# The last expert of a two-layer decoder in a written order: way back between the down products, final norm on ScalarE, stores of two batches

## The chip, the cores and the metric

The kernel runs on one core of a Trainium2 chip. The core has a matrix engine (TensorE, PE in the profile; its weight loads are listed as PEld), VectorE (DVE), ScalarE (ACT), GpSimd (POOL), and SyncE (SP), whose queue issues almost all DMA transfers here. The metric is the device time of one execution in microseconds (us), as the median of the runs; less is better.

## The reference

The input is 16 batches of 128 tokens with 256 features. Two decoder layers follow one another, each of three blocks (attention or mixture, cross attention, feed forward), and each block ends in `x = layernorm(x + block(x))`. The change is in the last block, a mixture of eight experts in which every expert picks its own tokens:

```python
logits = jnp.einsum('bsd,ed->bse', x, gate_w)
affinity = jnp.transpose(jax.nn.softmax(logits, axis=-1), (0, 2, 1))
gating, idx = jax.lax.top_k(affinity, k)              # k = S // E * CAPACITY = 32 tokens per expert and batch
x_in = x[bidx, idx]
h = jax.nn.silu(jnp.einsum('bekd,eid->beki', x_in, w_gate)) * jnp.einsum('bekd,eid->beki', x_in, w_up)
x_e = jnp.einsum('beki,edi->bekd', h, w_down)
out = jnp.zeros_like(x).at[bidx, idx].add(gating[..., None] * x_e)
...
x = _layernorm(x + out)      # mean and variance over the 256 features, eps 1e-5
```

## The kernel before

The last stage computes in float32, and the 16 tiles `x[b]` (128 tokens by 256 features) stay in SBUF for the whole kernel. `stage5` (line 2484) is the last stage. Its input `xin` holds, for each expert, the 512 picked tokens (32 of each of 16 batches), features on the partitions.

One expert goes as follows. `Results.hidden` (line 2456) runs eight times, once per 128 of the 1024 hidden units: products with the gate and up weights into the PSUM tiles `ps_g` and `ps_m` (line 2462), a SiLU on ScalarE (line 2466) and a product on VectorE (line 2467) that leaves `h`. `Results.down` (line 2469) runs four times, once per group g of four batches: eight matmuls over the hidden units into `ps_y` (line 2473), a copy to `y` on ScalarE (line 2474), and four small DMAs (line 2481). The rows of `y` are 4 batches by 32 tokens; the DMAs put the 32 rows of each batch into a tile `res.y[g]`, in which four experts come to lie above one another on the 128 partitions (they share the tag `ring` with other tiles, so the profile calls them `ring`).

The *way back* adds the experts' results to the tokens that they came from. For each batch one matmul with a gated one-hot matrix (`r.back`, called `half` in the profile) sums four experts at once into `ps_o` (line 2523), and VectorE adds it to `x[b]` (line 2524). It is done after expert 3 for experts 0 to 3 and after expert 7 for experts 4 to 7. After expert 7 each batch is then normed and stored: `K.layernorm` (line 85) takes statistics and their sum on VectorE (lines 88 and 90), the root on GpSimd in two instructions (lines 82 and 83, the second a power of -0.5), and scales on VectorE (line 93) into `o`; line 2528 stores `o` with a DMA of 128 KB per batch.

A float32 matmul of 128 by 256 shows as two MATMUL records in the trace, each with its weight load. I call one such record a pass.

What sets the order: outside of a block `tc.manual_schedule()` a scheduler of the framework orders the instructions of each engine by its own costs, and inside it they are issued as written. Each engine and the SP queue then work strictly in that order. `stage5` is scheduled by the framework before the change; the order that it chose puts the 32 down products of expert 7 first, then the 16 way-back products, and mixes adds, statistics and norms on VectorE. Tiles of one tag share a fixed number of buffers: `ps_o`, `ps_y`, `ps_g` and `ps_m` have two each, `o` two, `y` four.

Of the kernel before, what the change touches and what calls it, by code (L numbers as in the profile page):

```python
# [8 lines left out]
F32 = mybir.dt.float32  # L9
# [4 lines left out]
AF = mybir.ActivationFunctionType  # L14
ALU = mybir.AluOpType
# [4 lines left out]
P = 128  # L20
NB = 16
D = 256
# [5 lines left out]
class Kernel:  # L28
# [43 lines left out]
    def rows(self, pool, name, n):  # L72

        t = self.new(pool, [P, n], F32, name)
        self.nc.sync.dma_start(t, self.ins[name].partition_broadcast(P))
        return t
# [34 lines left out]
NE = 8  # L111
# [7 lines left out]
def stage0(K, early, ahead, late, late_dram, context):  # L119
# [8 lines left out]
    with ExitStack() as ctx:  # L128
# [560 lines left out]
        for n in range(N + 2):  # L689
# [24 lines left out]
            if mid:  # L714
                down(n - 1)
                factor(n - 1)
# [1609 lines left out]
TOK = 32  # L2326
FI = 1024


def load5(K, e, tile):  # L2330

    w = SimpleNamespace()
    w.gate, w.up, w.down = [], [], []
    for i, (n, dst) in enumerate((("l1f_gateT", w.gate), ("l1f_upT", w.up))):
        for k in range(KD):
            t = tile(2 * i + k, [P, FI])
            K.nc.sync.dma_start(t, K.ins[n][e][k * P:(k + 1) * P, :])
            dst.append(t)
    for i in range(2):
        t = tile(4 + i, [P, 4, D])  # L2340
        K.nc.sync.dma_start(t, K.ins["l1f_downT"][e].rearrange("(k p) n -> p k n", p=P)[:, 4 * i:4 * i + 4, :])
        w.down.append(t)
    return w
# [106 lines left out]
class Results:  # L2450
# [18 lines left out]
    def down(self, w, e, g, pd, y, rows):  # L2469

        K, nc = self.K, self.K.nc
        for c in range(FI // P):
            nc.tensor.matmul(pd, rows(c), w.down[c // 4][:, c % 4, :], start=(c == 0), stop=(c == FI // P - 1))  # L2473
        nc.scalar.copy(y, pd)  # L2474
        if e % 4 == 0:
            if g == 0:
                self.y = []
            self.y.append(K.new(self.ring, [P, 4, D], F32, "ring"))
        at = slice(e % 4 * TOK, e % 4 * TOK + TOK)
        for i in range(4):  # L2480
            nc.sync.dma_start(self.y[g][at, i, :], y[i * TOK:i * TOK + TOK, :])


def stage5(K, r, res, wp, first, out, ring):


    tc, nc = K.tc, K.nc
    x = K.x
    with ExitStack() as ctx:
        work = ctx.enter_context(tc.tile_pool(name="s5_work", bufs=2))  # L2490
        small = ctx.enter_context(tc.tile_pool(name="s5_small", bufs=4))
        ps = ctx.enter_context(tc.tile_pool(name="s5_ps", bufs=2, space=PSUM))


        def tile_of(i, shape):
            return K.new(wp, shape, F32, f"w5_{i}")

        weights = [first, load5(K, 1, tile_of)]
        for e in range(NE):
            w = weights[e]  # L2500
            hid = []
            n = 2 if e == 0 else 1
            wide = NB * TOK // n
            for c in range(0, FI // P, n):
                pg, pu = (K.new(ps, [P, n, wide], F32, t) for t in ("ps_g", "ps_m"))
                h = K.new(work, [P, n, wide], F32, "h", bufs=12)
                res.hidden(w, e, range(c, c + n), slice(NB * TOK - wide, NB * TOK), pg, pu, h)
                hid += [h[:, j, :] for j in range(n)]
            if e + 2 < NE:
                weights.append(load5(K, e + 2, tile_of))  # L2510
            for g in range(4 - 4 // n, 4):
                y = K.new(work, [P, D], F32, "y", bufs=4)
                at = (g - 4 + 4 // n) * P
                res.down(w, e, g, K.new(ps, [P, D], F32, "ps_y"), y, lambda c: hid[c][:, at:at + P])
            if e == 0:
                for g in range(4):
                    r.ways(g, small, ps, ring)
            if e % 4 < 3:
                continue
            for b in range(NB):  # L2520
                g, i = divmod(b, 4)
                po = K.new(ps, [P, D], F32, "ps_o")
                nc.tensor.matmul(po, r.back[g][:, i, e // 4, :], res.y[g][:, i, :], start=True, stop=True)
                nc.vector.tensor_tensor(x[b], x[b], po, ALU.add)
                if e == NE - 1:
                    o = K.new(work, [P, D], F32, "o")
                    K.layernorm(small, o, x[b])
                    nc.sync.dma_start(out[b], o)

# [1 line left out]
def decoder(tc, ins, out):  # L2533
    with ExitStack() as ctx:
# [5 lines left out]
        with ExitStack() as until4:  # L2540
# [37 lines left out]
            first = stage4(K, w.four, w.kv, r5, res)  # L2578
        p5 = pool(ctx, "w_5", bufs=2)
        stage5(K, r5, res, p5, first, out, w.kv.ring)  # L2580


# [60 lines left out]
```

## Time and profile before

| what | us |
|---|---|
| median of 3 runs | 1392.26 (1391.93 to 1396.34) |
| profiled execution, its own time | 1398.93 |
| its span, first to last instruction | 1397.1 |
| around the span (difference of the two) | 1.83 |
| mean granted TensorE clock | 0.957 |
| PE busy | 1231.7 (88%) |
| VectorE busy | 834.5 (60%) |
| ScalarE busy | 666.8 (48%) |
| GpSimd busy | 477.8 (34%) |

The profile is of one execution, 6.67 us longer than the median of the runs. Times in the timeline count from the first instruction. Busy shares are means over all stages, and say little of the last 40 us, which the change is in; those are read from the timeline, the chain of work that ended last, and tables by window. "Granted clock" is the share of full speed that the matrix engine was given in a window.

### The profile page before, as it was taken

How to read it: one execution, taken by the hardware profiler on the slowest of the kernel's cores; microseconds unless marked ns; L12 is line 12 of the kernel's file. 1: busy time of each engine (PE TensorE's matmuls, PEld its weight loads, DVE VectorE, ACT ScalarE, POOL GpSimd, SP SyncE). 2: the span in 40 equal slices, each digit the busy share in tenths (PEclk: the TensorE clock that was granted, in tenths of full speed). 3: DMA queues.
4: the chain of work that ended last, by engine and by line, in shares of the span. 5: the costliest groups of instructions: out<-in, count | busy, mean ns of one | idle time of the engine just before them, and what ended most of it. 6: DMA issues, size and time to landing. Idle time of an engine off the chain costs nothing.

```text
span 1397.1 us, 19300 instructions
## 1 busy us (share of the span) xinstructions
PE 1231.7 (88%) x6779; PEld 849.2 (61%) x6791; DVE 834.5 (60%) x1778; ACT 666.8 (48%) x1713; POOL 477.8 (34%) x642
## 2 busy tenths in 40 slices
PE   3688987889978999878898999998999999999995
PEld 1455444666654667656555788877777655666553
DVE  7899978989957898757444566667333111211115
ACT  5789865778956566543122665654521111111110
POOL 4256557668852776420042232332202000000003
PEclk9899988989999999997799999998999999999998
DMA  9368324111011211102000212211005222233002
GB/s 321 125 190 295 109 79 81 16 39 31 32 53 56 69 60 53 46 24 68 1 0 11 82 62 76 61 61 46 1 8 188 77 94 77 69 106 104 9 9 75
DMA packets 63121, 103.55 MB, mean 74 GB/s; under 512 B 11920, under 2 KB 41712, under 8 KB 62768
## 3 DMA queue, kind: packets, MB, share of 16 engines
q1 hardware_dynamic: 60848, 96.76, 20.8%
q0 software_dynamic: 2176, 5.55, 1.9%
q8 instruction: 54, 0.88, 0.3%
q14 instruction: 43, 0.35, 0.1%
HBM read 81.74 MB, written 16.35 MB: 70 GB/s over the span
## 4 chain that ended last, share of the span: by engine, by line
PE 52%; DVE 29%; ACT 7%; POOL 5%; issue 4%; DMA 2%; another core or an unknown queue 0%; SPq 0%; DVEq 0%; POOLq 0%; ACTq 0%
PE ps_y L2473 7%; PE ps_m L2462 7%; PE ps_g L2462 7%; PE ps_m L2018 4%; DVE acc L1307 3%; ACT s L2120 2%; PE ps_t L2140 2%; PE ps_m L2149 2%; PE ps_m L2038 2%; DVE cT L1316 2%; DVE s L915 1%; DVE m L2114 1%; DVE s L2110 1%; PE ps_t L2129 1%; PE ps_s L2107 1%
## 5 line engine op out<-in xcount | busy, mean ns | idle before, releaser
L2467 DVE TENSOR_TENSOR h<-h,ps_m 128x512 f32<-128x512 f32 x60 | 41.3, 688 | 228.4 <-PE ps_m L2462 228.4
L82 POOL TENSOR_SCALAR ln_t<-ln_mv 128x1 f32<-128x1 f32 (+1 forms) x84 | 16.4, 195 | 449.7 <-DVE ln_mv L90 308.4
L2120 ACT ACTIVATE s<-s,m 128x128 f32<-128x128 f32 x256 | 99.3, 390 | 69.1 <-DVE m L2114 69.1
L2466 ACT ACTIVATE h<-ps_g 128x512 f32<-128x512 f32 x60 | 35.8, 597 | 171.0 <-PE ps_g L2462 171.0
L2462 PE MATMUL ps_g<-xin,w 128*128 128x512 f32 x224 | 106.3, 592 | 0.0
L2462 PE MATMUL ps_m<-xin,w 128*128 128x512 f32 x224 | 105.3, 592 | 0.0
L2473 PE MATMUL ps_y<-w,h 128*128 128x256 f32 x448 | 97.8, 379 | 0.0
L2473 PEld LDWEIGHTS ps_y<-w,h 128*128 128x128 f32 x448 | 85.1, 190 | 14.6 <-issue 3.3
L2124 POOL TENSOR_TENSOR s<-s,t 128x1024 f32<-128x1024 f32 x32 | 60.7, 1896 | 91.1 <-DVE t L2123 91.1
L927 ACT ACTIVATE s<-s,m 128x128 f32<-128x128 f32 x256 | 83.2, 394 | 11.7 <-DVE m L922 11.7
L2462 PEld LDWEIGHTS ps_m<-xin,w 128*128 128x128 f32 x224 | 42.5, 190 | 51.4 <-issue 50.2
L2462 PEld LDWEIGHTS ps_g<-xin,w 128*128 128x128 f32 x224 | 42.0, 190 | 46.4 <-issue 45.0
L2018 PE MATMUL ps_m<-xT,half 128*128 128x256 f32 x256 | 62.5, 389 | 2.6 <-DVE qT L2023 1.9
L2474 ACT COPY y<-ps_y 128x256 f32<-128x256 f32 x30 | 11.2, 372 | 104.7 <-PE ps_y L2473 70.8
L2110 DVE TENSOR_TENSOR s<-ps_s,hide 128x1024 f32<-128x1024 f32 x32 | 39.2, 1224 | 35.9 <-PE ps_s L2107 35.9
L2149 PE MATMUL ps_m<-half,oT 128*128 128x256 f32 x256 | 59.3, 385 | 0.0
L1307 DVE SCALAR_TENSOR_TENSOR acc<-ps_m,l1a_conv_w,acc 128x508 f32<-128x508 f32 (+2 forms) x72 | 53.3, 740 | 3.0 <-ACT acc L1300 1.3
L2018 PEld LDWEIGHTS ps_m<-xT,half 128*128 128x128 f32 x256 | 47.4, 194 | 9.1 <-DVE qT L2023 2.3
L2149 PEld LDWEIGHTS ps_m<-half,oT 128*128 128x128 f32 x256 | 47.4, 190 | 7.5
L83 POOL TENSOR_TENSOR ln_rs<-ln_t,mhalf 128x1 f32<-128x1 f32 (+1 forms) x84 | 48.6, 578 | 7.0
L2120 ACT ACTIVATION_READ_ACCUMULATOR s<-s,m 128x1 f32 x256 | 48.1, 188 | 0.0
L1298 PE MATMUL ps_m<-xnT,l1a_in_proj 128*128 128x512 f32 x96 | 46.8, 611 | 0.4 <-ACT y L1268 0.4
(524 smaller groups left out, 3079.2 us busy)
## 6 DMA issues: line engine op xcount, KB each, us to landing
w<-in_w_gate_dram SPq DMA_DIRECT2D x9, 1024.0 KB
csb<-cs_dram SPq DMA_DIRECT2D x16, 512.0 KB
w<-in_l1f_gateT_dram SPq DMA_DIRECT2D x14, 512.0 KB
w<-in_l1f_upT_dram SPq DMA_DIRECT2D x14, 512.0 KB
w<-in_l1f_downT_dram SPq DMA_DIRECT2D x14, 512.0 KB
k<-kv SPq DMA_DIRECT2D x20, 256.0 KB
v<-kv SPq DMA_DIRECT2D x20, 256.0 KB
ring<-k SPq DMA_DIRECT2D x10, 512.0 KB
```

The source lines that it names most:

```text
L83: return self.nc.gpsimd.tensor_tensor(out, t, self.mhalf[: out.shape[0], :n], ALU.pow)
L927: nc.scalar.activation(at, at, AF.Exp, bias=m[h][:, i:i + 1])
L1298: nc.tensor.matmul(pc, w.inp[:, k, at:at + P], xnT[g][:, k, :], start=(k == 0), stop=(k == KD - 1))
L1307: nc.vector.scalar_tensor_tensor(accv[:, :, j:], pcv[:, :, :P - j], w.conv[:, c, TAPS - 1 - j:TAPS - j], accv[:, :, j:], ALU.mult, ALU.add,)
L2018: nc.tensor.matmul(pq[:, j, :], wt[k][:, at], src[:, k, :], start=(k == 0), stop=(k == KD - 1))
L2110: nc.vector.tensor_tensor(half(b, j), pss.rearrange("p r c k -> p (r c) k"), hide.unsqueeze(1).to_broadcast([P, 8, P]), ALU.add,)
L2120: nc.scalar.activation(at, at, AF.Exp, bias=m[j][:, i:i + 1], accum_out=t[j][:, i:i + 1])
L2124: nc.gpsimd.tensor_tensor(half(b, j), half(b, j), t[j].unsqueeze(2).to_broadcast([P, 8, P]), ALU.mult)
L2149: nc.tensor.matmul(py[b], oT[b][:, c, :], w.o[c // 4][:, c % 4, :], start=(c == 0), stop=(c == NC - 1))
L2462: nc.tensor.matmul(ps[:, j, :], m[k][:, c * P:(c + 1) * P], self.r.xin[:, k, e, cols], start=(k == 0), stop=(k == KD - 1),)
L2467: nc.vector.tensor_tensor(h, h, pu, ALU.mult)
L2473: nc.tensor.matmul(pd, rows(c), w.down[c // 4][:, c % 4, :], start=(c == 0), stop=(c == FI // P - 1))
```

## The change

The last expert leaves the loop and is written out in a block with a manual schedule. `Results.down` is split in two, of which the second half (`moved`) holds the four DMAs, without a change in what they do. The loop over the first seven experts keeps its text, and the way back of experts 0 to 3 stays where it was.

For the last expert, the order of groups is written by hand: the way back and the statistics of a group of four batches (`back`) stand behind the down products of the next group. The statistics of two batches go into one tile `ln_mv2`, and GpSimd computes the roots of two batches at once, then minus mean times root (two more instructions). ScalarE scales (`normed`) with the root as scale and that product as bias, instead of VectorE. Results of two batches lie in one `o` with four buffers, stored with one DMA of 256 KB (`stored`). For the last group, `begun` puts `x[b]` into PSUM with a product by the identity before the group's own down results have come, `back` adds the way back in the same PSUM tile, and statistics and scaling read PSUM; the add on VectorE is left out for these four batches.

```diff
-        for e in range(NE):
+        for e in range(NE - 1):
...
+        with tc.manual_schedule():
+            w, hid, po, o, todo = weights[NE - 1], [], {}, {}, []
...
+            def begun(g):
+                for b in range(4 * g, 4 * g + 4):
+                    po[b] = K.new(ps, [P, D], F32, "ps_g" if b % 2 else "ps_m")
+                    nc.tensor.matmul(po[b], K.ident, x[b], start=True, stop=False)
+
+            def back(g):
+                for i in range(4):
+                    b = 4 * g + i
+                    there = b in po
+                    if not there:
+                        po[b] = K.new(ps, [P, D], F32, "ps_o")
+                    nc.tensor.matmul(po[b], r.back[g][:, i, 1, :], res.y[g][:, i, :], start=not there, stop=True)
+                    if not there:
+                        nc.vector.tensor_tensor(x[b], x[b], po[b], ALU.add)
+                    of = po[b] if there else x[b]
+                    st = K.new(small, [P, 6], F32, "ln_st")
+                    nc.vector.bn_stats(st, of)
+                    if i % 2 == 0:
+                        mv = K.new(small, [P, 2, 2], F32, "ln_mv2")
+                    nc.vector.bn_aggr(mv[:, i % 2, :], st)
+                    if i % 2:
+                        rs, nb = (K.new(small, [P, 2], F32, t) for t in ("ln_rs2", "ln_nb2"))
+                        K.rsqrt(small, rs, mv[:, :, 1:2].rearrange("p h c -> p (h c)"), 1.0, 1e-5, "ln_t2")
+                        nc.gpsimd.tensor_tensor(nb, mv[:, :, 0:1].rearrange("p h c -> p (h c)"), rs, ALU.mult)
+                        nc.gpsimd.tensor_scalar(nb, nb, -1.0, None, ALU.mult)
+                        todo.append((b // 2, [po[b - 1 + j] if there else x[b - 1 + j] for j in range(2)], rs, nb))
+
+            def normed(g):
+                for _ in range(2):
+                    n, of, rs, nb = todo.pop(0)
+                    o[n] = K.new(work, [P, 2, D], F32, "o", bufs=4)
+                    for j in range(2):
+                        nc.scalar.activation(o[n][:, j, :], of[j], AF.Identity, scale=rs[:, j:j + 1], bias=nb[:, j:j + 1])
+
+            def stored(g):
+                for i in (2 * g, 2 * g + 1):
+                    nc.sync.dma_start(out[2 * i:2 * i + 2].rearrange("b p d -> p b d"), o[i])
+
+            down(0)
+            down(1)
+            back(0)
+            down(2)
+            normed(0)
+            back(1)
+            stored(0)
+            down(3)
+            normed(1)
+            back(2)
+            normed(2)
+            stored(1)
+            begun(3)
+            back(3)
+            stored(2)
+            normed(3)
+            stored(3)
```

More of the change, by code (lines that the diff above doesn't have):

```diff
@@ L2474, in down, with moved @@
         nc.scalar.copy(y, pd)
+        self.moved(e, g, y)
+    def moved(self, e, g, y):
+        K, nc = self.K, self.K.nc
         if e % 4 == 0:
@@ L2517, in stage5 @@
                     r.ways(g, small, ps, ring)
[L2518 to L2528, printed above, removed]
+            if e == 3:
+                for b in range(NB):
+                    g, i = divmod(b, 4)
+                    po = K.new(ps, [P, D], F32, "ps_o")
+                    nc.tensor.matmul(po, r.back[g][:, i, 0, :], res.y[g][:, i, :], start=True, stop=True)
+                    nc.vector.tensor_tensor(x[b], x[b], po, ALU.add)
@@ new lines, in stage5, with down @@
+        with tc.manual_schedule():
+            w, hid, po, o, todo = weights[NE - 1], [], {}, {}, []
+            for c in range(FI // P):
+                pg, pu = (K.new(ps, [P, 1, NB * TOK], F32, t) for t in ("ps_g", "ps_m"))
+                h = K.new(work, [P, 1, NB * TOK], F32, "h", bufs=12)
+                res.hidden(w, NE - 1, range(c, c + 1), slice(0, NB * TOK), pg, pu, h)
+                hid.append(h[:, 0, :])
+            def down(g):
+                y = K.new(work, [P, D], F32, "y", bufs=4)
+                res.down(w, NE - 1, g, K.new(ps, [P, D], F32, "ps_y"), y, lambda c: hid[c][:, g * P:(g + 1) * P])
+            def begun(g):
[49 more added lines that the diff above has]
+            stored(3)
```

## The prediction

> **What bounds the kernel now.** I read first the busy time in three windows of the last stage: the down products of expert 7, the way back, and what comes after the last matmul. Columns are busy time and instructions of each engine, granted clock, and DMA share.
>
> ```profile
> 1356.00:1370.60 14.60, 14.60 (x68) 12.47 (x67) 0.69 (x1) 1.12 (x3) 0.00 (x0) 1.00 0.09 25
> 1370.60:1386.00 15.40, 10.69 (x33) 5.75 (x31) 13.32 (x49) 0.37 (x1) 9.28 (x24) 0.89 0.24 80
> 1386.00:1397.00 11.00, 0.00 (x0) 0.00 (x0) 4.76 (x16) 0.00 (x0) 3.18 (x8) 0.67 0.28 96
> ```
>
> For 14 us only PE works; then VectorE (third figure) is nearly full for 15 us, and for 11 us more PE has nothing to do. Next I read the chain of work that ended last, over the same stretch (start, us, what).
>
> ```profile
> 1356.93 13.81 PE ps_y L2473 x64
> 1370.74 0.45 PE ps_o L2523 x2
> ...
> 1385.18 0.47 DVE ln_st L88 x2
> ...
> 1386.51 1.67 DMA out_dram<-o
> 1388.28 0.42 DVE o L93
> 1388.72 1.68 DMA out_dram<-o
> 1390.49 0.42 DVE o L93
> 1390.93 1.68 DMA out_dram<-o
> 1392.74 0.42 DVE o L93
> ```
>
> So the end is PE for 13.8 us, VectorE for some 15 us, then norms that each wait until an older store has landed and given back one of the two `o`. The last norm ends at 1393.67, the last store is issued at 1393.92 and lands at 1396.02, and closing work runs 1.05 us to 1397.07. Last, the groups of this stretch by form (busy, mean ns).
>
> ```profile
> L2473 PE MATMUL ps_y<-w,h 128*128 128x256 f32 x64 | 14.0, 379 | 0.0
> L2523 PE MATMUL ps_o<-ring,half 128*128 128x256 f32 x32 | 10.7, 459 | 4.7 <-DVE x L2524 4.6
> L83 POOL TENSOR_TENSOR ln_rs<-ln_t,mhalf 128x1 f32<-128x1 f32 x16 | 9.2, 573 | 1.3
> L93 DVE TENSOR_SCALAR o<-x,ln_mv,ln_rs 128x256 f32<-128x256 f32 x16 | 6.3, 407 | 4.1 <-DMA out_dram<-o 2.6 <-POOL ln_rs L83 1.3
> L2524 DVE TENSOR_TENSOR x<-x,ps_o 128x256 f32<-128x256 f32 x16 | 6.3, 396 | 13.7 <-PE ps_o L2523 13.7
> L88 DVE BATCH_NORM_STATS2 ln_st<-x 128x6 f32<-128x256 f32 x16 | 6.1, 407 | 0.0
> ```
>
> Matmuls overlap: 64 passes in 13.81 us are 0.2157 us each, whatever their 379 ns.
>
> **The change part by part.** The order in which the changed program issues its work is the same as before on every engine up to the down products of expert 7, and no table load is added on ScalarE. So everything up to 1363.68, the end of the second group's passes, is taken as it is, and I work forward from there.
>
> *Way back between the downs.* The results of group 0 are there: its four DMAs were issued from 1360.86 to 1362.68 and land 1.77 to 1.89 us later, at 1362.63, 1363.30, 1363.88 and 1364.52. Two matmuls go at once (two `ps_o`), 4 passes, 0.86 us. The third needs the first add: it comes 0.64 us after the matmul's start, takes 0.42, and PE follows 0.05 us later. The fourth needs the second add, and VectorE now has the statistics of one batch between two adds. A batch there is add 0.42 + 0.03, statistics 0.43 + 0.04, aggregate 0.08 until the next instruction starts (steps of dependent instructions at 1387.22 and at 699.28 of the timeline), 1.0 us. Fourth matmul at 0.64 + 1.0 + 0.42 + 0.05 = 2.11 us, its two passes 0.54 after a pause: 2.65 us per group of which 1.73 are passes. VectorE needs 4.0 us of each 6.1 us, so it isn't the bound. The sum on PE:
>
> - back(0) to 1366.33, down(2) with 16 passes (3.45) to 1369.78, back(1) to 1372.44, down(3) to 1375.89, back(2) to 1378.55.
> - begun(3), 8 passes that the old kernel doesn't have, 1.73, to 1380.27. It is covered: the last of the four DMAs of group 3 lands at 1375.67 + 0.46 (until ScalarE's copy) + 0.40 + 3.68 = 1380.21. Without it PE would wait about as long.
> - back(3) to 1382.0 in 8 passes, nothing to wait for but the matmuls before.
>
> *What is late next.* The adds of the last four batches are gone (4 x 0.42, paid for by begun(3)). Statistics run from 1380.9, 0.55 a batch, and end at 1383.2. GpSimd becomes the bound: for two batches it has 0.19 (line 82), the power, a product 0.20 and a scaling 0.19 (rows of 128 by 4: 199 and 193 ns), with 0.08 between two. The power of 128 by 2 is on no row; 128 by 1 takes 0.55, 128 by 4 takes 1.04. I take 0.71, on the line between them. That is 1.61 us for a pair from start to start. The sixth pair's statistics are there at 1380.54, so three pairs in a row end at 1380.63 + 3 x 1.61 - 0.08 = 1385.38, where VectorE alone would allow 1384.8.
>
> *ScalarE.* Two scalings of 128 by 256 with a scale per partition: rows between 372 ns (line 2474) and 489 ns (line 568), which start 0.31 to 0.42 us apart. I take 0.87 for two, to 1386.29. The other twelve lie under PE's work: normed(0) takes 1370.4 to 1372.1, before the copy of group 3 at 1376.13, which waits behind it on the same engine.
>
> *Stores.* SP has stored(0) ahead of group 3's four DMAs. It is done by some 1373.6, and SP needs them at 1376.5. With four `o` of two batches no scaling waits for a store. The last store carries 256 KB: stores of 128 KB land after 1.67 to 2.09 us, those of `k` with 256 KB after 2.00 to 2.64 us. I take 2.05. Another price stands in the Trainium skill ("DMA: Bandwidth & Descriptors", section on the anatomy of one DMA on the software path): 2.0 us plus the bytes over 436 GB/s, which is an estimated 2.6 us here and would make the sum 0.55 us less. It gives 2.3 for 128 KB, and these stores, on the hardware path, took 1.67 in most cases, so the row decides.
>
> **Sum**: 1386.29 + 0.03 + 2.05 + 1.05 = 1389.4 against 1397.1: 7.7 us less. The profiled execution would go from 1398.93 to 1391.2; its distance to the median, 6.67 us, lies mostly before this stage and stays. So 1392.26 - 7.7 = **1384.6**.
>
> Bounds: a group's way back on PE 2.4 to 2.9 (three of them, -0.75 to +0.75); the power 0.55 to 1.04 for three pairs (-0.5, then VectorE is the bound, to +1.0); the two small GpSimd steps up to 0.05 more each (+0.3); statistics from PSUM, for which there is no row: adds that read PSUM take 396 ns and statistics that read SBUF 407, so nothing to 0.1 each, hidden under GpSimd; two scalings 0.75 to 0.95 (+-0.1); the store 1.67 to 2.64 (-0.4 to +0.6). Together 5.0 to 9.4 us, so 1382.9 to 1387.3.
>
> **Rivals.** *The clock falls between the groups.* The clock goes in windows of 3.41 us.
>
> ```profile
> 1369.33:1372.74 3.41, 3.33 (x15) 2.26 (x13) 1.51 (x6) 0.37 (x1) 0.00 (x0) 1.00 0.14 39
> 1372.74:1376.15 3.41, 0.87 (x4) 0.38 (x3) 2.14 (x9) 0.00 (x0) 1.75 (x6) 1.00 0.21 67
> 1376.15:1379.57 3.42, 3.17 (x7) 1.89 (x8) 3.23 (x13) 0.00 (x0) 2.35 (x6) 0.50 0.27 94
> 1379.57:1382.98 3.41, 2.58 (x10) 1.40 (x9) 3.41 (x14) 0.00 (x0) 2.71 (x7) 1.00 0.29 100
> ```
>
> After a window with 4 passes and a pause of 2.2 us the next one got half the clock; after 7 and 10 passes the next was full. The new order has at least 8 passes in 2.65 us and 3.5 more of the downs, 11 a window, and no pause over 0.5 us. A DMA or add that is late by 2 us would break that. Each fallen window costs up to 1.7 us. Two of them: 1384.6 + 3.4 = 1388.0, at the edge of what can be told from no change.
>
> *The clock stays at half from the first way back on.* This is the case that ends slower. From 1363.68 PE has 72 passes, 15.5 us, which become 31.1, and the pauses (2.8 us) vanish in them: the last matmul 12.7 us later, GpSimd no longer the bound (-0.6): 1384.6 + 12.1 = 1396.7. It decides from five of the six windows on (5 x 1.7 over 7.7). The Trainium skill ("TensorE: Matmul & The Clock Gate", section on a second failure mode, by cycling PSUM buffers) says that short pauses between groups of matmuls can make the clock fall and rise again and again, which speaks against this order. The rows above don't show it: with pauses as short and fewer passes the clock came back and stayed.
>
> *A queue in front.* ScalarE does normed(0) before it copies group 3's `y`, and that copy releases the DMAs that back(3) needs. If the roots of pair 1 (1369.97 by my sum) came over 4 us late, all that follows would move with them; no row of GpSimd comes near that. A gain halved by such shifts: 1388.5.
>
> *More than forecast.* If PE doesn't pause in a group at all (1.73 instead of 2.65 us, three times) and the power costs as for one batch: 1384.6 - 2.8 - 0.5 = 1381.3. Against it stands that PE did wait for the adds before (4.6 us in the group row of line 2523).
>
> **How the numbers follow.** My forecast (1381.5 to 1387.5) 0.76; two windows of half clock or a gain halved by a queue 0.14; more than forecast, under 1381.5, 0.06; half clock throughout 0.04. What this kernel's measurement can tell from no change is about 0.3%, 4.2 us, so 1388.1 and 1396.4. Faster: 0.76 + 0.06 + half of 0.14 = 0.89, less 0.02 for the spread of the runs shown (their highest is 4.1 us over the median): 0.87. Same: 0.09. Slower: 0.04. Range 1381.5 to 1388.5, which takes in the bounds and half of the first rival.
>
> **What would show it.** Right: on PE some 2.65 us of way back after each of downs 1, 2 and 3; the last matmul ends near 1382.4, not 1386; no scaling waits for a store; GpSimd's eight powers of 128 by 2 at about 0.7 us, the last three pairs without a pause; last store issued near 1386.3; span near 1389.4. Wrong: half the clock in a window from 1366 on; PE waiting for a DMA at back(3); group 3's copy late behind the scalings; a power over 1.04 us.

## The result, and the profile after

| | before | after |
|---|---|---|
| median of 20 runs each, us | 1400.54 (1391.93 to 1410.26) | 1394.78 (1385.83 to 1401.72) |
| profiled execution: its own time, its span | 1398.93, 1397.1 | 1389.15, 1387.4 |
| mean granted clock in it | 0.957 | 0.961 |
| first down pass of the last expert, to the end of the span | 1356.77, 40.35 us | 1353.24, 34.20 us |

The ratio of the times is 0.9953, with a 95% interval of 0.9931 to 0.9974. By this ratio the kernel is 6.6 us faster (3.6 to 9.7), where 7.7 was forecast. But the predicted time of 1384.6 is missed by 10 us, and 1394.78 lies outside the range: the kernel before, with 1392.26 from three runs, has a median of 1400.54 over 20.

First the busy time of the changed kernel in three windows: the downs of the first groups with the first way back, the middle, and what is left from 1377.40 on (busy time and instructions of PE, PEld, DVE, ACT and POOL, then the granted clock, the DMA share and GB/s).

```profile
1353.24:1367.00 13.76, 13.39 (x61) 11.04 (x59) 4.60 (x14) 1.27 (x4) 2.65 (x8) 1.00 0.07 19
1367.00:1377.40 10.40, 9.60 (x42) 7.29 (x41) 7.44 (x25) 4.79 (x11) 4.13 (x13) 1.00 0.25 78
1377.40:1387.44 10.04, 1.22 (x6) 0.74 (x4) 2.07 (x8) 3.60 (x7) 3.75 (x12) 0.73 0.45 158
```

Before, VectorE had almost nothing to do during the downs and was nearly full during the way back. Now it works beside PE in the first two windows, and PE keeps the full clock up to its last passes. Then the chain of work that ended last (start, us, what).

```profile
1353.40 6.91 PE ps_y L2473 x32
1360.31 0.45 PE ps_o L2555 x2
1360.78 0.43 DVE x L2557
1361.24 0.44 DVE ln_st L2560
1361.70 0.18 DVE ln_mv L2563
1361.88 0.32 DVE x L2557
1362.24 0.70 PE ps_o L2555 x2
1362.94 3.45 PE ps_y L2473 x16
...
1380.69 0.20 POOL ln_t L82
1380.96 0.72 POOL ln_rs L83
1381.75 0.20 POOL ln_nb L2567
1381.99 0.27 POOLq L2709
1382.29 0.56 ACT o L2576
1382.85 0.46 ACTq L2709
```

PE for the downs, a short way back with two adds in it, the next downs; at the end GpSimd's operations of the last pair and ScalarE's scaling. (L2709 is the closing of the program. The view puts it where the pair's fourth operation and the second scaling ran.) No scaling in this chain follows a landing, and of VectorE's long stretch some 4 us are left, from 1366.86 to 1370.92 among the lines left out. The chain ends at 1383.31, so it doesn't tell what fills the last 4.1 us of the span; that is found below, under "What ends the program". The groups by form (busy, mean ns, idle before):

```profile
L2555 PE MATMUL ps_o<-ring,half 128*128 128x256 f32 x24 | 7.3, 405 | 1.2 <-DVE x L2557 0.9
L2576 ACT ACTIVATE o<-x,ln_nb,ln_rs 128x256 f32<-128x256 f32 x12 | 6.3, 592 | 2.8 <-POOL ln_nb L2568 2.8
L83 POOL TENSOR_TENSOR ln_rs<-ln_t,mhalf 128x2 f32<-128x2 f32 x8 | 5.6, 706 | 0.7
```

The power of 128x2 takes 706 ns, ScalarE's scaling 556 to 602 ns in its forms. In the list of waits (total, times, longest) the scalings wait for GpSimd's last operation of a pair alone, and none for a DMA:

```profile
ACT o L2576 <- POOL ln_nb L2568: 4.2, 4, 1.9
```

### The profile page after: what moved, and what is told of

Same layout as the page of the kernel before. It is cut to its first block, busy times and chain, and to the rows that moved or that the text cites. A ratio compares the mean times of both kernels' runs of the same rounds, so it can differ in the third digit from the quotient of the medians.

```text
span 1387.4 us, 19309 instructions
## 1 busy us (share of the span) xinstructions
PE 1228.2 (89%) x6799; PEld 846.6 (61%) x6799; DVE 830.5 (60%) x1758; ACT 675.3 (49%) x1729; POOL 476.1 (34%) x642
## 4 chain that ended last, share of the span: by engine, by line
PE 54%; DVE 28%; ACT 7%; POOL 5%; issue 4%; DMA 2%; SPq 0%; DVEq 0%; ACTq 0%; POOLq 0%
PE ps_m L2462 7%; PE ps_g L2462 7%; PE ps_y L2473 7%; PE ps_m L2018 5%; DVE acc L1307 3%; ACT s L2120 3%; PE ps_m L2149 2%; PE ps_t L2140 2%; PE ps_m L2038 2%; DVE cT L1316 2%; DVE m L2114 1%; DVE s L2110 1%; DVE s L915 1%; PE ps_s L2107 1%; PE ps_t L2129 1%
## 5 line engine op out<-in xcount | busy, mean ns | idle before, releaser
L82 POOL TENSOR_SCALAR ln_t<-ln_mv 128x1 f32<-128x1 f32 (+2 forms) x76 | 14.8, 194 | 444.1 <-DVE ln_mv L2563 292.8
L83 POOL TENSOR_TENSOR ln_rs<-ln_t,mhalf 128x1 f32<-128x1 f32 (+2 forms) x76 | 45.2, 594 | 6.3
```

The costliest lines, as they stand in the source:

```text
L83: return self.nc.gpsimd.tensor_tensor(out, t, self.mhalf[: out.shape[0], :n], ALU.pow)
```

## The experiments

All times here are counted from the first down pass of the last expert, since all up to there is the same work in every kernel, in the same order but for a few weight loads of an earlier stage; "stretch" is from there to the end of the span. The last two columns are what the runs led to: GpSimd's last operation, and that plus 5.13 us. Where the last column agrees with the stretch, GpSimd's end decides when the program ends.

| kernel | median, us | ratio to before, 95% | stretch | last scaling ends | GpSimd's last operation ends | + 5.13 |
|---|---|---|---|---|---|---|
| before | 1400.5 | 1 | 40.35 | 36.90 | 34.17 | 39.30 |
| changed | 1394.78 | 0.9953 (0.9931 to 0.9974) | 34.20 | 30.07 | 29.02 | 34.15 |
| after_again | 1394.72 | 0.9941 (0.9921 to 0.9960) | 34.22 | 30.06 | 29.00 | 34.13 |
| e1_eight_o | 1408.58 | 1.0043 (1.0013 to 1.0074) | 48.19 | 43.51 | 43.06 | 48.19 |
| e2_back_behind | 1397.18 | 0.9967 (0.9945 to 0.9990) | 36.74 | 32.66 | 31.61 | 36.74 |
| e3_norm_on_dve | 1395.84 | 0.9953 (0.9932 to 0.9973) | 34.05 | 29.95 | 28.92 | 34.05 |
| e4_no_begun | 1397.78 | 0.9966 (0.9947 to 0.9984) | 34.79 | 30.73 | 29.60 | 34.73 |
| e5_negate_on_dve | 1393.27 | 0.9948 (0.9927 to 0.9969) | 33.90 | 29.82 | 28.77 | 33.90 |
| e6_stores_of_one | 1393.63 | 0.9948 (0.9928 to 0.9967) | 34.13 | 30.05 | 29.00 | 34.13 |
| e7_one_o | 1403.95 | 1.0021 (1.0002 to 1.0041) | 43.02 | 39.81 | 29.57 | 34.70 |
| e8_late_gpsimd | 1397.06 | 0.9966 (0.9944 to 0.9987) | 35.49 | 30.06 | 30.35 | 35.48 |
| e9_sqrt | 1393.48 | 0.9926 (0.9898 to 0.9953) | 33.87 | 30.66 | (long before) | – |
| e10_last_group | 1392.19 | 0.9937 (0.9911 to 0.9963) | 32.43 | 28.54 | 25.39 | 30.52 |
| e11_root_single | 1396.99 | 0.9972 (0.9953 to 0.9990) | 37.98 | 33.44 | 32.85 | 37.98 |

Medians are of 4 to 20 runs (4 for e9_sqrt), and each ratio is to runs of the kernel before on the same chip. The intervals of most overlap; the stretch tells the kernels apart, because it repeats: 34.20 and 34.22 in two profiles of the changed kernel.

**The same kernel again.** No edit.

> The changed kernel once more, unedited. Measure: the last stretch, from the first down pass of expert 7 to the end of the span (before 40.4 us, after 34.2 us). Theory (the change takes 6 to 7 us out of the last stretch, and all else of a run's time is spread that the change has no part in, from how many 3.41 us windows of half clock fall into the earlier stages): last stretch 33.2 to 34.3 us; the start of the stretch moves by several us between profiles, by about half of the difference in half-clock time ahead of it; ratio to the kernel before 0.993 to 0.997. Rival (the profile caught a lucky execution and the stretch is itself spread): last stretch anywhere from 32 to 38 us, start of the stretch within 1 us of 1353.2.

Measured: stretch 34.22, though it begins at 1359.95, 6.7 us later than in the first profile of the same kernel. So in these two profiles the last stretch is the same to some hundredths of a microsecond, and what lies ahead of it is not. One part of the expectation failed: both profiles have the same 102.4 us at half clock ahead of the stretch, so half of that difference would have been no shift at all. Of the 6.7 us, 4.3 have gathered by 309 us, where the second profile spent 3.4 us less at half clock than the first; 3.1 come between 963 and 1063 us, where it spent 6.8 us more (in between it gained 0.7 back).

**One part alone: eight buffers for `o` in the kernel before.**

```diff
-                    o = K.new(work, [P, D], F32, "o")
+                    o = K.new(work, [P, D], F32, "o", bufs=8)
```

> The kernel before with eight buffers for the result tile o instead of two, nothing else. Theory (VectorE has 16 x 1.25 us to do after the last down pass, and waits for stores only on top of that): the stall at the end goes, last stretch 40.4 - 2.5 = 37.5 to 38.5 us. Rival (the two buffers are the whole story, the changed kernel is faster since no norm waits for a store): last stretch 34 to 35 us. Rival (stores are hidden anyway): 40 us.

Measured: 48.19 us, slower than all that was expected. The edit didn't do one thing alone: the framework's scheduler, with more buffers at hand, put each norm one operation behind its own aggregate, and VectorE then waits for GpSimd's root 16 times. The waits of this kernel, and its windows from the way back on:

```profile
DVE o L93 <- POOL ln_rs L83: 10.5, 16, 0.9
```

```profile
1371.00:1375.00 4.00, 2.15 (x8) 0.90 (x6) 2.72 (x10) 0.00 (x0) 1.48 (x4) 1.00 0.17 50
1375.00:1393.20 18.20, 11.76 (x22) 6.03 (x22) 11.80 (x42) 0.00 (x0) 7.38 (x20) 0.50 0.22 77
```

From 1375.0 on PE has 22 passes in 18.2 us and half the clock to the end. After the first add VectorE waits for nothing but the root, so it is its order that costs the time here, and not PE at half clock. This run says nothing on the buffers; it shows what the order of VectorE can cost, and beside it the falling clock of the rival, which the changed kernel escapes. The Trainium skill ("TensorE: Matmul & The Clock Gate", section on a second failure mode, by cycling PSUM buffers) tells of a kernel in which short idle times between groups of matmuls made the clock go up and down. Neither kernel here shows that: in the changed one, with waits of PE of at most 0.4 us, the clock stayed at 1.00 up to 1381.9; in this one, with waits of up to 2.2 us, it stayed at 0.50.

**The order alone undone.** The way back of all groups behind all downs, the rest as changed.

```diff
             down(1)
-            back(0)
             down(2)
-            normed(0)
-            back(1)
-            stored(0)
             down(3)
-            normed(1)
+            back(0)
+            normed(0)
+            stored(0)
+            back(1)
+            normed(1)
+            stored(1)
             back(2)
+            begun(3)
...
```

> The changed kernel with all four groups' way back behind all four groups' down products, the rest as it is (ScalarE scales, two batches per store, identity product for the last group, moved behind the third group's way back). Theory (VectorE without the scaling needs 12 x 1.0 + 4 x 0.55 us behind the downs, then the roots of the last two pairs, scaling, store): 13.8 + 0.6 + 12 + 2.2 + 2.2 + 1.1 + 2.1 + 1.1 = 35.1 us in the last stretch, so the written order is worth 1 to 2 us only and the scaling off VectorE most of the rest. Rival (the written order is what counts): 38 us or more.

Measured: 36.74, between the two expectations. In the chain, VectorE's batches now stand behind the downs, 0.98 us each, one behind another, until GpSimd takes over:

```profile
1375.14 0.32 DVE x L2557
1375.48 0.44 DVE ln_st L2560
1375.95 0.18 DVE ln_mv L2563
1376.13 0.32 DVE x L2557
1376.47 0.44 DVE ln_st L2560
1376.93 0.18 DVE ln_mv L2563
```

Undone alone, the written order is worth 2.5 us of the 6.15 by which the stretch became shorter; the other 3.6 stay without it.

**Scaling back on VectorE.**

```diff
...
-                        nc.gpsimd.tensor_tensor(nb, mv[:, :, 0:1].rearrange("p h c -> p (h c)"), rs, ALU.mult)
-                        nc.gpsimd.tensor_scalar(nb, nb, -1.0, None, ALU.mult)
...
-                        nc.scalar.activation(o[n][:, j, :], of[j], AF.Identity, scale=rs[:, j:j + 1], bias=nb[:, j:j + 1])
+                        nc.vector.tensor_scalar(o[n][:, j, :], of[j], mv[:, j, 0:1], rs[:, j:j + 1], ALU.subtract, ALU.mult)
```

GpSimd's two operations for the bias are left out, being no longer needed.

> The changed kernel with the scaling on VectorE again, as one subtract-and-multiply per batch in the same place of the order, so that GpSimd has two instructions per pair instead of four; order, stores and identity product as changed. Theory (VectorE has 4.0 + 1.3 us of work per group of 6.1 us, so it isn't the bound between the downs; the end loses GpSimd's queue of three pairs and gains VectorE's): last stretch within 1 us of the changed kernel, 33 to 34.5 us. Rival (taking the scaling off VectorE is what brings the gain): 37 us or more.

Measured: 34.05. With the order written, the two ways come out alike, since two things cancel: VectorE's last statistics end 1.0 us later (27.86 instead of 26.86), and GpSimd, with two operations a pair instead of four, still ends at 28.92 instead of 29.02. But something else showed: the last scaling ends 0.12 us earlier, the last store lands after 2.08 us instead of 3.01, yet the end comes only 0.15 us earlier. SP was ready 0.93 us before the closing began.

**What ends the program.** In the records of the trace, GpSimd has a long instruction called DRAIN behind its own work, and its end stands 4.345 us behind GpSimd's last operation in all 14 profiles, whatever that operation was; where it is the latest, closing takes 0.79 us more. That is the 5.13 us of the table. Four experiments on this. One adds a small operation at the end, whose result nobody uses:

```diff
             stored(3)
+            last = K.new(small, [P, 2], F32, "last")
+            nc.gpsimd.tensor_scalar(last, o[7][:, 1, :2], -1.0, None, ALU.mult)
```

> The changed kernel with one small operation more on GpSimd, of 128x2, that reads the last scaled batch and whose result nobody uses. Theory of the drain (the program ends no sooner than 4.35 us after GpSimd's last operation and 0.74 us of closing): the operation ends at about +30.4 us instead of GpSimd's last at +29.0, so 35.4 to 35.6 us instead of 34.2. Theory of the store, which the prediction had (the end is the last store's landing and 1.05 us): 34.2 us, no change.

```profile
1392.01 0.56 ACT L2576 ACTIVATE o<-ps_g,ln_nb,ln_rs 128x256 f32<-128x256 f32 x1
1392.59 0.37 SPq L2580 DMA_DIRECT2D out_dram<-o  x1
1392.64 0.21 POOL L2600 TENSOR_SCALAR last<-o 128x2 f32<-128x2 f32 x1 [1.13 <-ACT o L2576]
```

The timeline of that kernel's end: 0.21 us of work whose result nobody waits for, from 1392.64 to 1392.85, and the span ends at 1397.99, 5.13 us later. The stretch is 35.49 instead of 34.20. Neither the last scaling (30.06) nor the last store moved. So the end follows GpSimd's last operation, and the theory that the store alone sets it falls.

The second makes the stores half as large.

```diff
-                    nc.sync.dma_start(out[2 * i:2 * i + 2].rearrange("b p d -> p b d"), o[i])
+                    for j in range(2):
+                        nc.sync.dma_start(out[2 * i + j], o[i][:, j, :])
```

> The changed kernel with stores of one batch (128 KB) instead of two, the buffers as they are. Theory of the store (the end is the last landing and 1.05 us, as the prediction had it): the last 128 KB land in about 1.7 us instead of 2.1 to 3.0, so 33.0 to 33.8 us. Theory of the drain (GpSimd's last operation at +29.0, then 4.35 and 0.74 us): no sooner than 34.1 us, so 34.1 to 34.3 us, and the last store's landing leaves slack.

Measured: 34.13, as the drain has it. The size of the stores is worth nothing here, where GpSimd's end decides.

The third has GpSimd's chain once for each batch.

```diff
+                    if i % 2 == 0:
+                        rs, nb = (K.new(small, [P, 2], F32, t) for t in ("ln_rs2", "ln_nb2"))
+                    at = slice(i % 2, i % 2 + 1)
+                    K.rsqrt(small, rs[:, at], mv[:, i % 2, 1:2], 1.0, 1e-5, "ln_t1")
+                    nc.gpsimd.tensor_tensor(nb[:, at], mv[:, i % 2, 0:1], rs[:, at], ALU.mult)
+                    nc.gpsimd.tensor_scalar(nb[:, at], nb[:, at], -1.0, None, ALU.mult)
                     if i % 2:
-                        rs, nb = (K.new(small, [P, 2], F32, t) for t in ("ln_rs2", "ln_nb2"))
-                        K.rsqrt(small, rs, mv[:, :, 1:2].rearrange("p h c -> p (h c)"), 1.0, 1e-5, "ln_t2")
...
```

> The changed kernel with GpSimd's four operations made for each batch instead of for two (the arithmetic is the same). Theory that GpSimd's chain sets the end: about 1.2 us a batch (0.19, 0.55, 0.20, 0.22 and the gaps) instead of 1.61 a pair, statistics come every 0.98 us in the last group but one and every 0.55 in the last, so GpSimd runs without pause from +20.9 on and its last operation ends near +30.5 instead of +29.0; drain and closing give 35.4 to 36.2 us instead of 34.2. Rival (GpSimd is not what sets the end, the pairs are worth nothing): 34.0 to 34.4 us.

```profile
L83 POOL TENSOR_TENSOR ln_rs<-ln_t,mhalf 128x1 f32<-128x1 f32 x16 | 9.1, 567 | 1.3
L2569 POOL TENSOR_SCALAR ln_nb<-ln_nb 128x1 f32<-128x1 f32 x16 | 3.6, 224 | 1.4
L82 POOL TENSOR_SCALAR ln_t<-ln_mv 128x1 f32<-128x1 f32 x16 | 3.0, 190 | 286.5 <-DVE ln_mv L2563 285.3
L2568 POOL TENSOR_TENSOR ln_nb<-ln_mv,ln_rs 128x1 f32<-128x1 f32 x16 | 3.0, 190 | 1.3
```

Measured: 37.98. The mechanism is right, its size was set too low: the four operations are 1.17 us busy (567, 224, 190 and 190 ns), but one batch follows another after 1.50, not 1.2, since some 0.08 us lie between any two. So taking the roots of two batches at once is worth 3.8 us, more than the written order.

The fourth gives VectorE one of GpSimd's four operations.

```diff
-                        nc.gpsimd.tensor_tensor(nb, mv[:, :, 0:1].rearrange("p h c -> p (h c)"), rs, ALU.mult)
-                        nc.gpsimd.tensor_scalar(nb, nb, -1.0, None, ALU.mult)
+                        neg = K.new(small, [P, 2], F32, "ln_neg2")
+                        nc.vector.tensor_scalar(neg, mv[:, :, 0:1].rearrange("p h c -> p (h c)"), -1.0, None, ALU.mult)
+                        nc.gpsimd.tensor_tensor(nb, neg, rs, ALU.mult)
```

> The changed kernel with the mean negated by VectorE ahead of the root, so that GpSimd has three operations a pair instead of four (1.37 us instead of 1.61). Theory of GpSimd's chain: its last operation ends 0.3 to 0.9 us earlier (the last statistics, later by the negations, then bound it from the other side), and so does everything behind: 33.3 to 33.9 us instead of 34.2. Rival (VectorE, with 0.17 us more a pair, is late by as much as GpSimd gains): 34.1 us or more.

Measured: 33.90, 0.3 us less, at the edge of what was expected. The last statistics end at 27.44 instead of 26.86, so VectorE gives back most of what GpSimd gains.

**The buffers.** One `o` of two batches instead of four, the order on each engine unchanged.

```diff
-                    o[n] = K.new(work, [P, 2, D], F32, "o", bufs=4)
+                    o[n] = K.new(work, [P, 2, D], F32, "o", bufs=1)
                     for j in range(2):
                         ...
+                    nc.sync.dma_start(out[2 * n:2 * n + 2].rearrange("b p d -> p b d"), o[n])
...
             def stored(g):
-                for i in (2 * g, 2 * g + 1):
-                    nc.sync.dma_start(out[2 * i:2 * i + 2].rearrange("b p d -> p b d"), o[i])
+                pass
```

> The changed kernel with one buffer of two batches for the scaled result instead of four, which is as many bytes as the two buffers of one batch of the kernel before; each pair's store is issued right behind its scaling, the order on every engine stays. Theory of the buffers: each scaling waits for the store of the pair before, so a pair takes 1.0 (two scalings) + 0.1 + 2.2 (landing) = 3.3 us, and from the fourth pair on that chain sets the end: 40 to 41.5 us from the first down pass of the last expert to the end, against 34.2, so slower than the kernel before by about 0.5 us. Rival (the buffers cost nothing, GpSimd and the order set the pace): 34 to 35 us.

Measured: 43.02, slower than the kernel before. Its waits, and a piece of its chain:

```profile
ACT o L2576 <- DMA out_dram<-o: 17.5, 7, 3.9
```

```profile
1384.72 0.44 issue
1385.16 0.59 ACT o L2576
1385.76 0.02 issue
1385.77 2.07 DMA out_dram<-o
1387.84 0.02 issue
```

From the second pair on every pair waits for the landing of the one before, and a pair here takes 3.29 us (3.3 expected). The end is 1.5 us over the upper bound expected, since this chain begins with the first pair and not with the fourth. With one buffer the rest of the change is worth less than nothing: enough buffers are a condition for it. One buffer makes scaling and landing take turns, though, and two buffers of one batch, as the kernel before had them, weren't tried in the new order.

**The last group's x in PSUM, undone.**

```diff
-            begun(3)
             back(3)
```

> The changed kernel without the four passes that bring the last group's x into PSUM: x is added by VectorE again. Counted from the first down pass of the last expert (the changed kernel: 34.20 and 34.22 us to the end of the span). My theory: VectorE then needs some 0.98 instead of 0.55 us a batch for the last four, so the last statistics end about 0.7 us later, and GpSimd's last pair, which otherwise waits behind the pair before it, 0.3 to 0.5 us later: 34.4 to 34.8 us, ratio to the kernel before about 0.9955. Rival (these passes also hold TensorE's clock and cover the last DMAs, so without them the way back is late): above 35.5 us. Rival (they only delay): below 34.0 us.

Measured: 34.79, as expected, with the last statistics at 27.97 instead of 26.86. Those eight passes are worth 0.6 us.

**GpSimd out of the norm.**

```diff
...
-                        K.rsqrt(small, rs, mv[:, :, 1:2].rearrange("p h c -> p (h c)"), 1.0, 1e-5, "ln_t2")
-                        nc.gpsimd.tensor_tensor(nb, mv[:, :, 0:1].rearrange("p h c -> p (h c)"), rs, ALU.mult)
-                        nc.gpsimd.tensor_scalar(nb, nb, -1.0, None, ALU.mult)
...
+                        nc.vector.tensor_scalar(t, mv[:, :, 1:2].rearrange("p h c -> p (h c)"), 1e-5, None, ALU.add)
+                        nc.vector.reciprocal(t, t)
+                        nc.scalar.activation(rs, t, AF.Sqrt)
...
-                        nc.scalar.activation(o[n][:, j, :], of[j], AF.Identity, scale=rs[:, j:j + 1], bias=nb[:, j:j + 1])
+                        nc.vector.tensor_scalar(o[n][:, j, :], of[j], mv[:, j, 0:1], rs[:, j:j + 1], ALU.subtract, ALU.mult)
```

> The changed kernel with GpSimd taken out of the last norm: VectorE adds the 1e-5 and takes the reciprocal, ScalarE the square root, VectorE scales. If GpSimd's pair chain (1.61 us a pair) and its drain set the end, the last pair is scaled about 0.7 us (two small operations, a square root, handing over) + 0.75 us (two scalings) behind the last statistics at about +27, so the last store is issued near +28.5, lands 2.1 us later, and 1.1 us close: 31 to 32.3 us instead of 34.2, ratio to the kernel before 0.993 to 0.994. Rival (VectorE, with statistics, roots and scalings of 16 batches, becomes the bound as soon as GpSimd is not): 33.5 us or more. Rival (ScalarE changes its function tables for each square root among its copies): above 35 us.

Measured: 33.87, so the rival was right: VectorE is the next bound. The rival of the function tables didn't come: ScalarE loaded a table once in the stretch (1.283 us, at 7.54), not for each root. Its timeline ahead of the last group's statistics:

```profile
1386.19 1.38 DVE L2577 TENSOR_SCALAR o<-x,ln_mv,ln_rs 128x256 f32<-128x256 f32 x4
1387.49 0.43 DVE L2560 BATCH_NORM_STATS2 ln_st<-ps_m 128x6 f32<-128x256 f32 x1
```

Four scalings of the group before stand in front of the last group's statistics, which end at 28.45 instead of 26.86. Here the store ends the program: 1.10 us from its landing to the end.

**Both bounds moved.** Only the last two pairs are taken off GpSimd, and their scalings are split over two engines.

```diff
+            nc.scalar.activation(K.new(small, [P, 1], F32, "early"), K.ident[:, :1], AF.Sqrt)
...
-                        mv = K.new(small, [P, 2, 2], F32, "ln_mv2")
+                        mv = K.new(small, [P, 2, 2], F32, "ln_mv2", bufs=8)
...
+                        if there:
+                            t = K.new(small, [P, 2], F32, "ln_t2")
+                            nc.vector.tensor_scalar(t, mv[:, :, 1:2].rearrange("p h c -> p (h c)"), 1e-5, None, ALU.add)
+                            nc.vector.reciprocal(t, t)
...
+            def normed_last():
+                (m, pf, r6, nb, mv6, t6), (n, of, r7, _, mv7, t7) = todo
+                o[m], o[n] = (K.new(work, [P, 2, D], F32, "o", bufs=4) for _ in range(2))
+                nc.scalar.activation(r6, t6, AF.Sqrt)
+                nc.scalar.activation(r7, t7, AF.Sqrt)
+                nc.vector.scalar_tensor_tensor(nb, mv6[:, :, 0:1].rearrange("p h c -> p (h c)"), -1.0, r6, ALU.mult, ALU.mult)
+                for j in range(2):
+                    nc.scalar.activation(o[m][:, j, :], pf[j], AF.Identity, scale=r6[:, j:j + 1], bias=nb[:, j:j + 1])
+                    nc.vector.tensor_scalar(o[n][:, j, :], of[j], mv7[:, j, 0:1], r7[:, j:j + 1], ALU.subtract, ALU.mult)
```

> The changed kernel with the last group alone taken off GpSimd: VectorE adds 1e-5 and takes the reciprocal for the last two pairs (0.17 us each operation), ScalarE takes the square roots (0.20 us, its function table loaded early by a square root of one column that nobody uses), ScalarE scales the last pair but one and VectorE the last. GpSimd's last operation is then that of the pair before, near +25.6 us from the first down pass of the last expert, and with 4.35 + 0.74 us its drain allows an end at +30.7, so the store decides: last statistics at +26.7, two small operations and the root to +27.4, scalings on both engines to +28.5, landing 2.1 us, closing 1.1 us: 31.5 to 32.2 us against 34.2 of the changed kernel, and a ratio to the kernel before of about 0.992. Rival (VectorE, loaded with the small operations, is late with its statistics as in the kernel with GpSimd out of the whole norm, where the last ones ended at +28.45): 33.3 us or more.

```profile
1388.21 0.55 ACT L2593 ACTIVATE o<-ps_m,ln_nb,ln_rs 128x256 f32<-128x256 f32 x1
1388.34 0.54 DVE L2594 TENSOR_SCALAR o<-ps_m,ln_mv,ln_rs 128x256 f32<-128x256 f32 x1 [0.21 <-ACT ln_rs L2590]
1388.66 0.55 ACT L2593 ACTIVATE o<-ps_g,ln_nb,ln_rs 128x256 f32<-128x256 f32 x1
1388.80 0.54 DVE L2594 TENSOR_SCALAR o<-ps_g,ln_mv,ln_rs 128x256 f32<-128x256 f32 x1
```

Measured: 32.43, 1.8 us less than the changed kernel and 0.2 over what was expected, mostly since the two last stores are ready together and SP issues one 0.46 us behind the other. The scalings end at 28.54 as forecast, GpSimd would allow 30.5, and the store sets the end. Its stretch is the shortest of those tried, in one profile: its last store landed after 2.31 us, and a late landing, such as ended the stretch of the changed kernel (3.01), would have taken up to 0.7 us of the gain. Its median is 1392.19, and the interval of its ratio overlaps that of the changed kernel.

## Why the prediction was wrong in the time and right in most of its steps

**The step that failed** is the last of the sum: "its distance to the median, 6.67 us, lies mostly before this stage and stays. So 1392.26 - 7.7 = 1384.6." The profiled execution of 1398.93 was no outlier; the median of three runs was. The kernel before took 1400.54 as the median of 20 runs, and 1402.70, 1401.94 and 1400.25 in three later groups of 27, 25 and 31 runs, on three chips. Of all these runs none but the first two was as quick as 1392.26. From 1400.54 the same sum gives 1392.8, two below what was measured. The four times that were to be had (1391.93, 1392.26, 1396.34, 1398.93) spread over 7 us, as much as the whole change was to bring, and the range had no term for that: it took only "0.02 for the spread of the runs shown" off a chance. Half of those 7 us more at the upper end (1392.0) would still have missed by 2.8 us; a range around the profiled execution instead of the median would have been nearer.

What moves the base is ahead of the change. In the 14 profiles the last expert's downs begin between 1352.42 and 1368.29 us, though the work ahead of them is the same; the time that PE spent at half the clock until there goes from 92.2 to 133.1 us, and the two go together (correlation 0.90, 0.35 us per microsecond at half clock). It isn't all of it: the two profiles of the changed kernel have 102.4 us each and begin 6.7 us apart. Over 212 runs, each against the mean of its own kernel, the time falls by some 8 us for each 0.01 of mean granted clock (correlation -0.77). That is a connection between records, not an experiment; what decides how many such stretches an execution gets, what else moves the start, and why two of the first three runs were so quick, wasn't tried and stays open.

**The gain** was forecast as 7.7 us with bounds of 5.0 to 9.4; measured were 6.15 in the stretch and 6.6 by the ratio. The 1.55 us between forecast and stretch are the terms of the sum: GpSimd 0.40, the scalings 0.15, the landing of the last store 0.96 (3.01 instead of 2.05), the closing 0.05. But the store's two terms hide a second bound, as the point on the end tells. The steps of the sum, with the changed kernel's times shifted by the 3.53 us by which its stretch began earlier:

- *PE* was right: down(2) began at 1362.78 (1362.80 by the sum), back(2) at 1372.31 (1372.36), the last pass at 1378.24 (1378.25). A way back between downs took 2.6 to 2.7 us (2.65), PE never waited for a DMA, and the clock stayed full.
- *The power of 128x2*: 0.71 forecast, 0.706 measured. *The pair*: 1.61 forecast, 1.64 measured without a pause.
- *"The last three pairs without a pause"* was wrong, and GpSimd ended 0.40 us late. The first of the three began 0.1 us late, a pair took 0.03 more than forecast, and before the second GpSimd stood still for 0.28 us instead of 0.08, because VectorE's first aggregate of the last group had waited for GpSimd:

```profile
DVE ln_mv L2563 <- POOL ln_rs L83: 0.5, 1, 0.5
```

  With eight buffers for these statistics (e10) that wait isn't in the list, which points at the buffers, but that kernel differs in more than that.
- *ScalarE's two scalings*: 0.87 forecast, from rows of other operations; 1.02 measured. Scale and bias from tensors cost 0.56 to 0.60 us an instruction, more than any row that I had bounded it by.
- *The end*: 1386.29 + 0.03 + 2.05 + 1.05 lets the last store alone set the end. That mechanism was incomplete, and a tie hid it. The last store of the first profile landed late, after 3.01 us (15 of its 16 completions had come by 2.11), and 1.10 us closed, which gives 34.20; GpSimd's drain gives 34.15 of its own, so a store landing on time would have saved only 0.05. With GpSimd at 1385.38, as forecast, drain and closing would have given 1390.5 instead of 1389.4, a gain of 6.6 us. In the kernel before the drain couldn't be seen: there it allowed an end 1.05 us ahead of the store's.
- *The price of a store.* The Trainium skill ("DMA: Bandwidth & Descriptors", section on the anatomy of one DMA on the software path) gives an estimated 2.6 us for 256 KB. The 88 stores of 256 KB in the profiles, all on the hardware path, took 2.06 to 2.42 in 70 cases and 2.66 to 3.59 in the others. The row was the better guide for most; the last store of the first profile (3.01) fell outside its bound of 2.64. (By the page the gain would have been 0.55 us less and the end as much later; the prediction says "the sum".)
- *The rivals.* Neither the falling clock nor the queue in front of group 3's copy came: the clock stayed full until 1381.9, behind PE's last pass, and ScalarE copied group 3 at 1372.55, right behind its downs.

What the parts are worth, each undone by itself: the buffers 8.8 us, the roots of two batches at once 3.8, the written order 2.5, x in PSUM 0.6, stores of two batches and the engine of the scaling about nothing (-0.1 and -0.15). They don't add up to 6.15, since undoing one of them also changes what the others are worth; the buffers undone alone cost more than the whole change brought.

## What to carry to other kernels

A gain in one stage could be worked out here from one profile to within 1.6 us, but the absolute time rests on a base, and three runs are not one: set the range by the spread of all executions at hand, the profiled one included. At the end of a program look at the last operation of every engine, not only at the last store: here 0.2 us of work on GpSimd, for nobody, made the program 1.3 us longer, because it ended 1.3 us after GpSimd's other work. Before you move work to a written order, ask what the freed engines will wait for next: buffers, then the engine with the most instructions a batch, then the end itself.

## What the runs showed of the hardware

- GpSimd's drain at the end takes 4.345 us from the end of its last operation, the same to 1 ns in 14 profiles (4.345 or 4.346), after a power (before), a product of two columns (after) or a product of 128x256 (e9).
- GpSimd's small operations cost mostly by the instruction: four of one column take 1.50 us from batch to batch (e11), four of two columns 1.64 (after).
- Statistics read PSUM as quickly as SBUF (399 to 414 ns against 427, after), but VectorE's scaling of a PSUM tile takes 0.54 us where one of SBUF takes 0.41 (e9).
- A store of 256 KB is late now and then (18 of 88 landed after 2.66 to 3.59 us, the others after 2.06 to 2.42), often by one of its 16 completions: in the changed kernel's last store 15 came by 2.11 us and one after 3.01.
